# Collecting the spread of y about its first channel, and moving the sums of wo behind the first expert

## The chip, the cores and the metric

The kernel runs on one core of one Trainium2 chip. The metric is the device time of one execution in microseconds (us). The median of three runs of the kernel before is 2669.09 us (2668.46 to 2669.94). One more execution was taken with the hardware profiler; all rows shown come from it.

## The reference

All values are float32. There are B = 4 batches of S = 1024 tokens with D = 1024 channels. Cut to what matters:

```python
xn = layernorm(x)
# linear attention
q, v = xn @ Wq, xn @ Wv                    # 16 heads, lam = sigmoid(beta) per head
state[t] = lam * state[t-1] + v[t]         # along the tokens
y = q * state
mu, var = mean(y), var(y)                  # over the 1024 channels of a token
y = (y - mu) * rsqrt(var + 1e-5) * ln_g + ln_b
y = y * silu(xn @ Wg)
attention = y @ Wo
# mixture of 64 experts, top 8 per token, at most 128 tokens of an expert
w, idx = top8(softmax(xn @ router.T)), w / sum(w)
for each expert e, on its tokens xg:
    h = silu(xg @ w1[e]) * (xg @ v1[e])    # 384 hidden channels
    out[tokens] += w * (h @ w2[e])
x + attention + out
```

## The kernel before

**Layout.** In the attention, channels lie on the 128 partitions and tokens on the free axis. A channel group c of 128 channels (c = 0 to 7) is one tile y(c) of 128 x 1024, so the mean and the variance of a token are sums over eight tiles and then over 128 partitions. The sum over partitions is a matmul with a constant matrix whose elements are all 1/1024 (`all_channels`, L596 to L602, the tile `mean_w`); its result is the same in all partitions.

**Block products.** Every large product of matrices is done as a two by two block product with seven block products in place of eight. `left_sums` (L49 to L54) and `right_sums` (L57 to L68) form the sums and differences of blocks, `steps` (L130 to L175) runs the seven products: PSUM banks a, b and c take them, ACT copies partial results out (`copied`, L148: s1, s5 and s2), and DVE adds them (L160, L169, L172). A copy by ACT must be done before PE's next product may go on into the same bank: pc's second product waits for s5, and pa's next product for s2. `product` (L178) starts one product's first parts, finishes the product before (`before()`), and may put other work (`late`) ahead of its last parts.

**Per batch** (`batch_row`, L582). For m = 0 to 3, `states(m)` makes v and its scan and `queries(m)` multiplies q by it: this gives y(m) and y(m + 4). Then come four `gates(m)`, with silu of the gate, the layernorm of y (L680, L681, L684) and the DMAs of the gated y to DRAM (L689, from POOL's queue). `find_spread` (L655) is the `late` work of gates(0): it gives mean and 1/sqrt(var + eps).

**How the spread is collected before.** After queries(0) `find_shift` (L633) takes the mean of the first and fifth channel group, a quarter of the channels: POOL adds y(0) and y(4) (L644), PE sums over partitions (`sh`, two matmuls, L599), ACT scales (L636). This shift is subtracted from every y in place on DVE (L624). ACT squares the shifted y (L626, L629), POOL adds the squares into sum2 (L630) and the values into sum1 (L631). `find_spread` forms the mean from sum1, its square (L661), the variance from sum2 (L664), the root (L665, ACT, with a table load) and the reciprocal (L666, DVE). The shift keeps the difference of two large squares small.

**The experts** (`Experts`, L827). For expert e, `hidden(e)` runs the two products with w1 and v1 (L890), silu on ACT (L895) and the product on DVE (L896) into a tile of which there is one (tag "cur"). `fetch(e + 2)` loads the weights and gathers the tokens with indirect DMAs from POOL's queue (L857, L864). `turned(e + 1)` transposes the next tokens on DVE (L875). `output(e - 1)` transposes act on PE (hpt, L905), copies it (hT, L906, DVE), multiplies by w2 (L911), scales (L914) and adds to the output by an indirect DMA (L922). Between them stand the parts of the output projection y @ Wo (`project`, pa_o, pb_o, pc_o), 16 units spread over the experts. `load_wo` (L931) loads the four blocks of Wo and forms their sums on DVE at once.

**What sets the order.** A scheduler of the framework orders the instructions of each engine by its own estimates. Where `in_order` (L79) is used, the named engines keep the order of the program. For the first three experts that is DVE alone (L976). Semaphores between engines follow from the tiles that they share, and a tile that is to be reused waits for its last reader.

Of the kernel before, what the change touches and what calls it, by code (L numbers as in the profile page):

```python
# [8 lines left out]
F32 = mybir.dt.float32  # L9
I32 = mybir.dt.int32  # L10
AF = mybir.ActivationFunctionType
ALU = mybir.AluOpType
# [4 lines left out]
P = 128  # L17
B, S, D = 4, 1024, 1024
NTOK = B * S
KD = D // P  # L20
KH = KD // 2
SH = S // 2
NM = SH // P
# [22 lines left out]
H0, H1 = slice(0, SH), slice(SH, S)  # L46
# [10 lines left out]
def right_sums(eng, blocks, new, keep=False):  # L57


    t3 = blocks["T3"] = new("T3")  # L60
    eng.tensor_tensor(t3, blocks["B22"], blocks["B12"], ALU.subtract)
    b12 = blocks["B12"] if keep else blocks.pop("B12")
    t1 = blocks["T1"] = new("T1") if keep else b12
    eng.tensor_tensor(t1, b12, blocks["B11"], ALU.subtract)
    t2 = blocks["T2"] = new("T2")
    eng.tensor_tensor(t2, blocks["B22"], t1, ALU.subtract)
    t4 = blocks["T4"] = new("T4")
    eng.tensor_tensor(t4, blocks["B21"], t2, ALU.subtract)  # L68
# [29 lines left out]
class Pools:  # L98
# [21 lines left out]
    def y(self, name):  # L120
        return self.three.tile([P, 3, S], F32, tag="y", name=name)
# [111 lines left out]
def attn_and_routing(  # L233
# [3 lines left out]
    nc = tc.nc  # L237
    one, line, scratch, small = pools.one, pools.line, pools.scratch, pools.small
# [22 lines left out]
    eps = one.tile([P, 1], F32, name="eps")  # L261
# [320 lines left out]
    def batch_row(b, left):  # L582
# [3 lines left out]
        ys = [pools.y(f"y_{b}_{i}") for i in range(3)]  # L586

        def y(c, cols=slice(0, S)):
            return ys[place[c] // 3][:, place[c] % 3, cols]

        shift = mean = ys[2][:, 2, :]
        sum1 = one.tile([P, S], F32, tag="sum1", name=f"sum1_{b}")
        sum2 = one.tile([P, S], F32, tag="sum2", name=f"sum2_{b}")
        spread = []

        def all_channels(t, h, name):  # L596

            ps = pools.bank("r", [P, SH], name)
            nc.tensor.matmul(  # L599
                ps, lhsT=mean_w, rhs=t[:, h * SH : (h + 1) * SH], start=True, stop=True  # L600
            )
            return ps  # L602

        def states(m, left, late):

            lo = line.tile([P, S], F32, tag="line", name=f"lo_{b}_{m}")
            hi = line.tile([P, S], F32, tag="line", name=f"hi_{b}_{m}")

            def then(c21):
                scan(lo, lo, m, 0.0)  # L610
                scan(hi[:, H0], c21, m + KH, 0.0)
                scan(hi[:, H1], hi[:, H1], m + KH, hi[:, SH - 1 : SH])

            left = product(
                nc, pools, weights(b, 0, m), quarters[b],
                lo[:, H0], lo[:, H1], hi[:, H1], then, left, f"v_{b}_{m}", late,
                begun.get(0) if b == 0 and m == 0 else None,
            )
            return lo, hi, left

        def queries(m, lo, hi, left):
            def less_shift():
                for i, c in enumerate((m, m + KH)):
                    nc.vector.tensor_tensor(y(c), y(c), shift, ALU.subtract)  # L624
                    if m == 0 and i == 0:
                        nc.scalar.activation(sum2, y(c), AF.Square)  # L626
                        continue
                    sq = line.tile([P, S], F32, tag="line", name=f"sq_{b}_{c}")
                    nc.scalar.activation(sq, y(c), AF.Square)  # L629
                    nc.gpsimd.tensor_tensor(sum2, sum2, sq, ALU.add)  # L630
                    nc.gpsimd.tensor_tensor(sum1, y(0) if m == 0 else sum1, y(c), ALU.add)  # L631

            def find_shift():  # L633
                for h, cols in enumerate((H0, H1)):
                    ps = all_channels(sum1, h, f"sh_{b}_{h}")
                    nc.scalar.activation(shift[:, cols], ps, AF.Copy, scale=float(NM))  # L636
                less_shift()

            def then(c21):
                nc.vector.tensor_tensor(y(m + KH, H0), c21, hi[:, H0], ALU.mult)  # L640
                nc.vector.tensor_tensor(y(m), y(m), lo, ALU.mult)
                nc.vector.tensor_tensor(y(m + KH, H1), y(m + KH, H1), hi[:, H1], ALU.mult)
                if m == 0:
                    nc.gpsimd.tensor_tensor(sum1, y(0), y(KH), ALU.add)  # L644
                else:
                    less_shift()

            left = product(
                nc, pools, weights(b, 1, m), quarters[b],
                y(m, H0), y(m, H1), y(m + KH, H1), then, left, f"q_{b}_{m}", None,  # L650
                begun.get(1) if b == 0 and m == 0 else None,
            )
            return left, find_shift if m == 0 else None

        def find_spread():  # L655

            for h, cols in enumerate((H0, H1)):
                ps = all_channels(sum1, h, f"mean_{b}_{h}")
                nc.scalar.copy(mean[:, cols], ps)
            rstd = one.tile([P, S], F32, tag="sum1", name=f"rstd_{b}")  # L660
            nc.scalar.activation(rstd, mean, AF.Square)  # L661
            for h, cols in enumerate((H0, H1)):
                ps = all_channels(sum2, h, f"var_{b}_{h}")
                nc.vector.tensor_tensor(rstd[:, cols], ps, rstd[:, cols], ALU.subtract)  # L664
            nc.scalar.activation(rstd, rstd, AF.Sqrt, bias=eps)  # L665
            nc.vector.reciprocal(rstd, rstd)  # L666
            spread.append(rstd)

# [28 lines left out]
                find_spread if m == 0 else None,  # L697
            )

        late = None  # L700
        taking = take(b)
        for m in range(NM):
            lo, hi, left = states(m, left, late)
            if b == 0 and m == 0:
                for tokens in later:
                    store(*tokens)

                for to in (rows[NTOK:NROW, :], wtab[NTOK:NROW, :], out[NTOK:NROW, :]):
                    tc.keep_in_program_order(
                        nc.gpsimd.dma_start(out=to, in_=zero[:, 0 : to.shape[1]])  # L710
                    )
            next(taking)
            left, late = queries(m, lo, hi, left)
            next(taking)
            if b + 1 < B:
                if m == 1:
                    prep(b + 1, 0)
                elif m == 2:
                    load_turned(b + 1, 0)
                    route(b + 1, 0, folded(b + 1, 0, scored(b + 1, 0)))  # L720
            if m == NM - 1:
                tc.keep_in_program_order(
                    nc.sync.dma_start(
                        out=out[b * S : (b + 1) * S, :], in_=x[b * S : (b + 1) * S, :]
                    )
                )
# [3 lines left out]
        for m in range(NM):  # L730
# [8 lines left out]
            left = gates(m, left)  # L739
# [82 lines left out]
    for b in range(B):  # L822
        left = batch_row(b, left)
# [3 lines left out]
class Experts:  # L827
# [103 lines left out]
    def load_wo(self):  # L931
        for name, (i, o) in zip(("B11", "B21", "B22", "B12"), BLOCKS):
            self.wo_b[name] = self.pools.block(f"wo_{name}")
            load_block(self.nc, self.wo_b[name], self.wo, i, o * SH, SH)
        right_sums(self.nc.vector, self.wo_b, lambda n: self.pools.block(f"wo_{n}"))

    def load_gated(self, u):
        t = self.pools.left.tile([P, NSLOT, KH, P], F32, tag="w", name=f"gated_{u}")
# [23 lines left out]
        self.turn = self.turned(0)  # L962

    def run(self):
        units = B * NM
        gated = self.load_gated(0)
        self.fetch(1)
        self.load_wo()
        self.load(0, 2)


        begins = [1 + u * (E - 4) // units for u in range(units)] + [E - 3]
        before, todo, u, many = None, None, 0, iter(())
        for e in range(E):

            kept = [mybir.EngineType.DVE] if e < 3 else []  # L976
            with in_order(self.tc, kept):
                act = self.hidden(e, self.turn)
                self.fetch(e + 2)
                self.load(e + 1, 2)  # L980
                if e + 1 < E:
                    self.turn = self.turned(e + 1)
                if before is not None:
                    self.output(*before)
                before = e, act
                if u < units and e == begins[u]:
                    todo = self.project(u, gated)
                    many = iter((3, 2, 2) if begins[u + 1] - e == 3 else (2, 2, 2, 1))
                    u += 1
                    gated = self.load_gated(u) if u < units else None  # L990
                for _ in range(next(many, 0)):
                    next(todo, None)
        self.output(*before)
# [48 lines left out]
```

## Time and profile before

| what | value |
|---|---|
| median of three runs | 2669.09 us (2668.46 to 2669.94) |
| profiled execution | 2671.9 us, span 2670.1 us |
| mean granted clock of PE | 0.997 |
| PE busy | 2642.0 us, 99% |
| DVE busy | 1082.8 us, 41% |
| ACT busy | 330.8 us, 12% |
| POOL busy | 737.5 us, 28% |
| chain that ended last | PE 95%, DVE 3%, DMA 1% |

The span runs from the first to the last instruction of the profiled execution, and that execution's own time is 1.8 us longer. PE is the tensor engine, DVE the vector engine, ACT the scalar engine, POOL is GpSimd and SP issues DMAs. In a timeline row there are the start and the length in us, the engine, the line of the program, the operation, what it writes and reads, and in square brackets the idle time ahead of it with what ended it. In a group's row there are the busy time of all in us, the mean of one in ns and the idle time ahead. In a row of windows, after the stretch and its length, come the busy times of PE, PE's weight loads, DVE, ACT and POOL, with the number of instructions, and then the granted clock of PE, the share of the DMA engines and GB/s. A float32 matmul appears as two records.

### The profile page before, as it was taken

Reading aid. Unit: us, or ns where it says so; the run is one execution under the profiler, and the core shown is the slowest. Engines: PE = TensorE matmul, PEld = TensorE weight load, DVE = VectorE, ACT = ScalarE, POOL = GpSimd, SP = SyncE. Lnnn points to the kernel's source line nnn. Section 1 sums busy time; section 2 is a strip of 40 time slices with the busy share of each in tenths; the row PEclk is TensorE's granted clock in tenths of the full one; section 3 lists DMA queues with packets and bytes.
Section 4 is the critical chain, followed back from the end, with each engine's and each line's share of the span. In section 5 each row is a group of like instructions: output and inputs, shape, how many; then the busy total and the mean of one; then the engine's idle time right before and its main releaser. Section 6 shows DMA issues by size and latency. Waiting matters only on the chain.

```text
span 2670.1 us, 18675 instructions
## 1 busy us (share of the span) xinstructions
PE 2642.0 (99%) x6981; PEld 1272.4 (48%) x6981; DVE 1082.8 (41%) x1426; ACT 330.8 (12%) x492; POOL 737.5 (28%) x655
## 2 busy tenths in 40 slices
PE   9999999999999999999999999999999999999997
PEld 5444444444444444444555555555555555555554
DVE  7945676464943676373222212222122221222221
ACT  4213112131212211121000000000000000000000
POOL 1453312121122102132333323333233332333321
PEclk9999999999999999999999999999999999999999
DMA  6555534443335432326889888898888988889876
GB/s 236 194 182 194 193 107 144 179 156 110 123 110 210 166 116 83 145 98 239 296 284 305 283 274 284 285 304 283 274 284 284 305 283 273 284 286 303 270 272 181
DMA packets 122474, 592.95 MB, mean 222 GB/s; under 512 B 15872, under 2 KB 52736, under 8 KB 89360
## 3 DMA queue, kind: packets, MB, share of 16 engines
q1 hardware_dynamic: 81488, 448.03, 46.1%
q0 software_dynamic: 40464, 143.72, 19.9%
q8 instruction: 55, 0.90, 0.1%
q14 instruction: 35, 0.29, 0.0%
q10 hardware_dynamic: 432, 0.01, 0.0%
HBM read 483.67 MB, written 124.81 MB: 228 GB/s over the span
## 4 chain that ended last, share of the span: by engine, by line
PE 95%; DVE 3%; DMA 1%; issue 0%; ACT 0%; POOL 0%; SPq 0%; POOLq 0%; DVEq 0%; ACTq 0%
PE h L890 25%; PE y L911 12%; PE pa_o L137 8%; PE pa_g L137 8%; PE pa_v L137 7%; PE pa_q L137 7%; PE pc_o L137 4%; PE pc_q L137 4%; PE pc_g L137 4%; PE pc_v L137 4%; PE pb_g L137 2%; PE pb_o L137 2%; PE pb_v L137 2%; PE pb_q L137 2%; PE lg L475 1%; PE hpt L905 1%
## 5 line engine op out<-in xcount | busy, mean ns | idle before, releaser
L890 PE MATMUL h<-w,xgT 128*128 128x384 f32 x2048 | 672.2, 486 | 0.7 <-issue 0.7
L890 PEld LDWEIGHTS h<-w,xgT 128*128 128x128 f32 x2048 | 388.9, 190 | 286.1 <-issue 33.6
L857 POOL DMA_INDIRECT xg<-rows,tables x256 | 252.6, 987 | 669.4 <-DVE xgT L875 603.7
L911 PE MATMUL y<-w,hT 128*128 128x512 f32 x768 | 343.6, 597 | 1.6 <-DVE hT L906 1.6
L906 DVE COPY hT<-hpt 128x384 f32<-128x384 f32 x64 | 35.6, 557 | 724.5 <-PE hpt L905 724.5
L137 PE MATMUL pa_g<-xT,w 128*128 128x512 f32 x512 | 233.9, 600 | 2.9 <-DVE ghi L172 2.9
L911 PEld LDWEIGHTS y<-w,hT 128*128 128x128 f32 x768 | 140.9, 190 | 192.6 <-issue 153.3
L137 PE MATMUL pa_q<-xT,w 128*128 128x512 f32 x480 | 216.5, 593 | 2.0 <-DVE y L172 2.0
L137 PE MATMUL pa_v<-xT,w 128*128 128x512 f32 x480 | 217.4, 593 | 0.0
L137 PE MATMUL pa_o<-wo_T,gated 128*128 128x512 f32 x384 | 177.7, 592 | 0.0
L914 DVE TENSOR_SCALAR ys<-y,wt 128x512 f32<-128x512 f32 x128 | 95.9, 749 | 200.1 <-PE y L911 197.6
L137 PEld LDWEIGHTS pa_g<-xT,w 128*128 128x128 f32 x512 | 97.9, 192 | 127.3 <-issue 123.4
L137 PEld LDWEIGHTS pa_q<-xT,w 128*128 128x128 f32 x480 | 90.6, 190 | 114.6 <-issue 110.5
L137 PEld LDWEIGHTS pa_v<-xT,w 128*128 128x128 f32 x480 | 90.6, 190 | 114.5 <-issue 112.9
L895 ACT ACTIVATE act<-h 128x384 f32<-128x384 f32 x64 | 31.5, 492 | 848.5 <-PE hpt L905 833.2
L922 POOL DMA_INDIRECT out_dram<-ys,tables x63 | 102.5, 1627 | 112.0 <-DMA out_dram<-ohi 83.8
L689 POOL DMA_DIRECT2D gated<-y x64 | 48.2, 758 | 254.1 <-DVE y L684 242.3
L137 PE MATMUL pc_o<-wo_B,gated 128*128 128x512 f32 x256 | 117.1, 592 | 0.0
L137 PE MATMUL pc_g<-xT,w 128*128 128x512 f32 x256 | 115.3, 593 | 1.5 <-ACT sc_g L148 1.5
L137 PE MATMUL pc_v<-xT,w 128*128 128x512 f32 x256 | 115.4, 593 | 0.7 <-ACT sc_v L148 0.7
L137 PE MATMUL pc_q<-xT,w 128*128 128x512 f32 x256 | 115.5, 592 | 0.0
L631 POOL TENSOR_TENSOR sum<-sum,y 128x1024 f32<-128x1024 f32 x24 | 56.9, 2373 | 205.2 <-DVE y L624 205.2
(209 smaller groups left out, 2499.2 us busy)
## 6 DMA issues: line engine op xcount, KB each, us to landing
w<-in_w_dram SPq DMA_DIRECT2D x128, 1536.0 KB
w<-in_v_dram SPq DMA_DIRECT2D x64, 1536.0 KB
w<-wsum SPq DMA_DIRECT2D x36, 1792.0 KB
wsum<-w POOLq DMA_DIRECT2D x12, 1792.0 KB
x<-in_x_dram SPq DMA_DIRECT2D x32, 512.0 KB
rows<-x POOLq DMA_DIRECT2D x32, 512.0 KB
gated<-y POOLq DMA_DIRECT2D x64, 256.0 KB
gated<-gated SPq DMA_DIRECT2D x16, 1024.0 KB
```

The lines of the kernel that those rows point to most:

```text
L137: nc.tensor.matmul(ps, lhsT=lhs[:, slot, k, :], rhs=blocks[right][:, k, :], start=start and k == 0, stop=stop and k == KH - 1, skip_group_ ...
L475: nc.tensor.matmul(two[i * E : (i + 1) * E, :], lhsT=r_sb[:, i * KH + k, :], rhs=blocks[f"B{i + 1}{h + 1}"][:, k, :], start=(k == 0), stop ...
L631: nc.gpsimd.tensor_tensor(sum1, y(0) if m == 0 else sum1, y(c), ALU.add)
L689: nc.gpsimd.dma_start(out=gated[b, :, :, slot, m, :].rearrange("u p j -> p u j"), in_=yc[:, h * SH : (h + 1) * SH].rearrange("p (u j) -> p ...
L857: nc.gpsimd.indirect_dma_start(out=xg[:, r, :], out_offset=None, in_=self.rows.rearrange("n (q c) -> (n q) c", q=NQ), in_offset=bass.Indir ...
L890: nc.tensor.matmul(ps, lhsT=xT[:, k, :], rhs=w[:, k, :], start=(k == 0), stop=(k == KD - 1))
L895: nc.scalar.activation(act, ph[0], AF.Silu)
L905: nc.tensor.transpose(pt[:, j, :], act[:, j * P : (j + 1) * P], self.ident)
L906: nc.vector.tensor_copy(hT, pt)
L911: nc.tensor.matmul(ps, lhsT=hT[:, j, :], rhs=w2[:, j, cols], start=(j == 0), stop=(j == KF - 1))
L914: nc.vector.tensor_scalar(ys[:, cols], ps, wt, None, ALU.mult)
L922: self.nc.gpsimd.indirect_dma_start(out=to, out_offset=bass.IndirectOffsetOnAxis(ap=rows, axis=0), in_=ys, in_offset=None, compute_op=ALU.add,
```

## The change

Three things are changed.

1. The shift is gone. Each y(c) except y(0) has y(0) subtracted, on DVE, into a tile of its own (`away`), which is squared on ACT. POOL adds the squares into sum2 and the unshifted y into sum1. So in each partition the spread is collected about the value of that partition's first channel.
2. `find_spread` pools the partitions: from sum1 and y(0) it forms, with two subtractions on DVE and two squares on ACT, what has to be taken from and added to sum2 so that the sum over partitions is the variance about the common mean. The square of the mean and the subtraction from PSUM are gone; ACT takes the root from PSUM in two halves. In the changed kernel's own numbering the lines are: away L625, its square L626, the adds L628 and L629, the first off L650, its square L651, sum2 - off L652, the mean's matmuls and copies L655, the second off L656, its square L657, sum2 + off L658, var and its root L662, the reciprocal L663, and the subtraction of the mean from y L677.
3. The sums of the blocks of Wo move from `load_wo` into the first expert, behind the transposition of the second expert's tokens. For the first three experts PE is now kept in the order of the program, as DVE was.

```diff
--- before.py
+++ after.py
@@ -588,7 +588,7 @@
         def y(c, cols=slice(0, S)):
             return ys[place[c] // 3][:, place[c] % 3, cols]
 
-        shift = mean = ys[2][:, 2, :]
+        mean = ys[2][:, 2, :]
         sum1 = one.tile([P, S], F32, tag="sum1", name=f"sum1_{b}")
         sum2 = one.tile([P, S], F32, tag="sum2", name=f"sum2_{b}")
         spread = []
@@ -601,7 +601,7 @@
             )
             return ps
 
-        def states(m, left, late):
+        def states(m, left):
 
             lo = line.tile([P, S], F32, tag="line", name=f"lo_{b}_{m}")
             hi = line.tile([P, S], F32, tag="line", name=f"hi_{b}_{m}")
@@ -613,56 +613,53 @@
 
             left = product(
                 nc, pools, weights(b, 0, m), quarters[b],
-                lo[:, H0], lo[:, H1], hi[:, H1], then, left, f"v_{b}_{m}", late,
+                lo[:, H0], lo[:, H1], hi[:, H1], then, left, f"v_{b}_{m}", None,
                 begun.get(0) if b == 0 and m == 0 else None,
             )
             return lo, hi, left
 
         def queries(m, lo, hi, left):
-            def less_shift():
-                for i, c in enumerate((m, m + KH)):
-                    nc.vector.tensor_tensor(y(c), y(c), shift, ALU.subtract)
-                    if m == 0 and i == 0:
-                        nc.scalar.activation(sum2, y(c), AF.Square)
-                        continue
-                    sq = line.tile([P, S], F32, tag="line", name=f"sq_{b}_{c}")
-                    nc.scalar.activation(sq, y(c), AF.Square)
-                    nc.gpsimd.tensor_tensor(sum2, sum2, sq, ALU.add)
-                    nc.gpsimd.tensor_tensor(sum1, y(0) if m == 0 else sum1, y(c), ALU.add)
-
-            def find_shift():
-                for h, cols in enumerate((H0, H1)):
-                    ps = all_channels(sum1, h, f"sh_{b}_{h}")
-                    nc.scalar.activation(shift[:, cols], ps, AF.Copy, scale=float(NM))
-                less_shift()
+            def collect(c):
+
+                away = line.tile([P, S], F32, tag="line", name=f"away_{b}_{c}")
+                nc.vector.tensor_tensor(away, y(c), y(0), ALU.subtract)
+                nc.scalar.activation(sum2 if c == KH else away, away, AF.Square)
+                if c != KH:
+                    nc.gpsimd.tensor_tensor(sum2, sum2, away, ALU.add)
+                nc.gpsimd.tensor_tensor(sum1, y(0) if c == KH else sum1, y(c), ALU.add)
 
             def then(c21):
                 nc.vector.tensor_tensor(y(m + KH, H0), c21, hi[:, H0], ALU.mult)
                 nc.vector.tensor_tensor(y(m), y(m), lo, ALU.mult)
                 nc.vector.tensor_tensor(y(m + KH, H1), y(m + KH, H1), hi[:, H1], ALU.mult)
-                if m == 0:
-                    nc.gpsimd.tensor_tensor(sum1, y(0), y(KH), ALU.add)
-                else:
-                    less_shift()
+                for c in (m, m + KH):
+                    if c > 0:
+                        collect(c)
 
             left = product(
                 nc, pools, weights(b, 1, m), quarters[b],
                 y(m, H0), y(m, H1), y(m + KH, H1), then, left, f"q_{b}_{m}", None,
                 begun.get(1) if b == 0 and m == 0 else None,
             )
-            return left, find_shift if m == 0 else None
+            return left
 
         def find_spread():
 
+
+            off = line.tile([P, S], F32, tag="line", name=f"off_{b}")
+            nc.vector.scalar_tensor_tensor(off, y(0), -float(KD), sum1, ALU.mult, ALU.add)
+            nc.scalar.activation(off, off, AF.Square, scale=KD**-0.5)
+            nc.vector.tensor_tensor(sum2, sum2, off, ALU.subtract)
             for h, cols in enumerate((H0, H1)):
                 ps = all_channels(sum1, h, f"mean_{b}_{h}")
                 nc.scalar.copy(mean[:, cols], ps)
+            nc.vector.scalar_tensor_tensor(off, sum1, 1.0 / KD, mean, ALU.mult, ALU.subtract)
+            nc.scalar.activation(off, off, AF.Square, scale=KD**0.5)
+            nc.vector.tensor_tensor(sum2, sum2, off, ALU.add)
             rstd = one.tile([P, S], F32, tag="sum1", name=f"rstd_{b}")
-            nc.scalar.activation(rstd, mean, AF.Square)
             for h, cols in enumerate((H0, H1)):
                 ps = all_channels(sum2, h, f"var_{b}_{h}")
-                nc.vector.tensor_tensor(rstd[:, cols], ps, rstd[:, cols], ALU.subtract)
-            nc.scalar.activation(rstd, rstd, AF.Sqrt, bias=eps)
+                nc.scalar.activation(rstd[:, cols], ps, AF.Sqrt, bias=eps)
             nc.vector.reciprocal(rstd, rstd)
             spread.append(rstd)
 
@@ -697,10 +694,9 @@
                 find_spread if m == 0 else None,
             )
 
-        late = None
         taking = take(b)
         for m in range(NM):
-            lo, hi, left = states(m, left, late)
+            lo, hi, left = states(m, left)
             if b == 0 and m == 0:
                 for tokens in later:
                     store(*tokens)
@@ -710,7 +706,7 @@
                         nc.gpsimd.dma_start(out=to, in_=zero[:, 0 : to.shape[1]])
                     )
             next(taking)
-            left, late = queries(m, lo, hi, left)
+            left = queries(m, lo, hi, left)
             next(taking)
             if b + 1 < B:
                 if m == 1:
@@ -932,7 +928,6 @@
         for name, (i, o) in zip(("B11", "B21", "B22", "B12"), BLOCKS):
             self.wo_b[name] = self.pools.block(f"wo_{name}")
             load_block(self.nc, self.wo_b[name], self.wo, i, o * SH, SH)
-        right_sums(self.nc.vector, self.wo_b, lambda n: self.pools.block(f"wo_{n}"))
 
     def load_gated(self, u):
         t = self.pools.left.tile([P, NSLOT, KH, P], F32, tag="w", name=f"gated_{u}")
@@ -962,7 +957,7 @@
         self.turn = self.turned(0)
 
     def run(self):
-        units = B * NM
+        nc, units = self.nc, B * NM
         gated = self.load_gated(0)
         self.fetch(1)
         self.load_wo()
@@ -973,13 +968,15 @@
         before, todo, u, many = None, None, 0, iter(())
         for e in range(E):
 
-            kept = [mybir.EngineType.DVE] if e < 3 else []
+            kept = [mybir.EngineType.DVE, mybir.EngineType.PE] if e < 3 else []
             with in_order(self.tc, kept):
                 act = self.hidden(e, self.turn)
                 self.fetch(e + 2)
                 self.load(e + 1, 2)
                 if e + 1 < E:
                     self.turn = self.turned(e + 1)
+                if e == 0:
+                    right_sums(nc.vector, self.wo_b, lambda n: self.pools.block(f"wo_{n}"))
                 if before is not None:
                     self.output(*before)
                 before = e, act
```

## The prediction

> **What bounds the kernel now.** I read the engine shares first, then the chain of work that ended last.
>
> ```profile
> PE 2642.0 (99%) x6981; PEld 1272.4 (48%) x6981; DVE 1082.8 (41%) x1426; ACT 330.8 (12%) x492; POOL 737.5 (28%) x655
> ...
> PE 95%; DVE 3%; DMA 1%; issue 0%; ACT 0%; POOL 0%; SPq 0%; POOLq 0%; DVEq 0%; ACTq 0%
> ```
>
> TensorE is busy for 2642.0 of 2670.1 us. So an edit is worth what it takes from TensorE or from its few gaps, and it costs what it adds to either. Next I listed PE's gaps. Apart from the start and the tail, the ones above half a microsecond are 0.66, 1.48, 0.56, 1.00, 1.00, 0.68, 2.90, 0.71, 0.65, 0.65 and 0.98. The largest is in the timeline of PE and DVE where the attention hands over to the experts, and the window there shows the clock:
>
> ```profile
> 1242.53 2.29 DVE L61 TENSOR_TENSOR wo_T<-wo_B,wo_B 128x2048 f32<-128x2048 f32 x1 [10.23 <-DMA wo_B<-in_wo_dram]
> 1244.73 0.68 DVE L169 TENSOR_TENSOR glo<-pc_g,sc_g 128x512 f32<-128x512 f32 x1
> 1245.33 2.28 DVE L64 TENSOR_TENSOR wo_B<-wo_B,wo_B 128x2048 f32<-128x2048 f32 x1
> ...
> 1248.27 6.66 PE L137 MATMUL pa_g<-xT,w 128*128 128x512 f32 x8 [2.90 <-DVE ghi L172]
> ...
> 1248.00:1249.00 1.00, 0.73 (x1) 0.50 (x2) 1.00 (x2) 0.63 (x1) 0.00 (x0) 0.50 0.00 0
> 1250.00:1251.00 1.00, 1.00 (x3) 0.34 (x2) 1.00 (x1) 0.00 (x0) 1.00 (x2) 0.50 0.00 0
> ```
>
> DVE waits for the DMA of wo and then does its sums ahead of glo and ghi of the last gates; PE waits 2.90 us, and its next eight records last 6.66 us (3.43 elsewhere), at clock 0.50. By the clock of each microsecond, the half rate began about 1.9 us into the gap and lasted 6.85 us.
>
> **The change, part by part.**
>
> *The shift goes (gain).* The group to read is
>
> ```profile
> L599 PE MATMUL sh<-sum,mean_w 128*128 128x512 f32 x16 | 8.6, 616 | 0.0
> ```
>
> Sixteen records are eight matmuls. Eight records take 3.43 us in the chain, so a matmul takes 0.858 and eight take 6.87 us. No gap stands before them: **-6.87**. The eight ACT copies at L636, four of 32 subtractions at L624 and eight POOL adds (15 a batch become 13, 2.35 us each) go too. They run beside PE: nothing.
>
> *The pooled spread (loss).* The new find_spread (L650 to L663 and L677 below are the changed kernel's lines) adds on DVE `off` (L650), `sum2-off` (L652), a second `off` (L656) and `sum2+off` (L658), and two ACT squares (L651, L657); it drops the old square L661 and subtractions L664. DVE is 41% busy and ACT 12%, so the time itself hides. The queue positions do not. In the compiled order, in batches 1 and 2, ACT takes L651 ahead of its copies s5 (from pc_g) and s2 of the first gates; in batch 3 ahead of s2; in batch 0 behind both. L651 waits for `off`, which waits for POOL's last add to sum1, and behind it on ACT stand the copies that free PSUM for PE. Batch 1 before:
>
> ```profile
> 546.51 2.34 POOL L631 TENSOR_TENSOR sum<-sum,y 128x1024 f32<-128x1024 f32 x1
> 548.82 2.34 POOL L630 TENSOR_TENSOR sum<-sum,sq 128x1024 f32<-128x1024 f32 x1
> ...
> 548.88 3.43 PE pa_g L137 x8
> 552.31 3.43 PE pc_g L137 x8
> ```
>
> In the new order POOL's last sum1 add is the one that takes the place of 546.51, so it ends at 548.85, and the last add to sum2 follows at once, to 551.2. `off` reads two tiles from SBUF on DVE. What that meets is seen here:
>
> ```profile
> 237.14 5.87 DVE L624 TENSOR_TENSOR y<-y 128x1024 f32<-128x1024 f32 x1
> ...
> 236.67 2.34 POOL L630 TENSOR_TENSOR sum<-sum,sq 128x1024 f32<-128x1024 f32 x1
> 238.97 0.57 POOL L571 DMA_DIRECT2D wsum<-w  x1
> 239.55 2.37 POOL L631 TENSOR_TENSOR sum<-sum,y 128x1024 f32<-128x1024 f32 x1
> ```
>
> An operation of 1.22 us lasted 5.87, until POOL's adds were over. [...] If POOL starts first: `off` 551.2 to 552.5, square 1.06 to 553.6, s5's copy 0.59 to 554.15, against 552.31 when pc_g is due: 2.0 late, and 0.15 at var_0 (mean copy, L656, two subtractions L677 and L658 are 6.1 us, against 6.0 of matmuls placed there). If DVE starts first: 551.8, in time. POOL needs no semaphore from another engine there, so I take it as first: 2.15 each, **+4.3** for batches 1 and 2 (ends 0.3 and 4.3).
>
> Batch 3: POOL works through the token DMAs until 1162.27, so sum1 is ready at 1164.65, and pa_g is due at 1165.66:
>
> ```profile
> 1162.28 2.37 POOL L631 TENSOR_TENSOR sum<-sum,y 128x1024 f32<-128x1024 f32 x1
> 1164.58 2.38 POOL L630 TENSOR_TENSOR sum<-sum,sq 128x1024 f32<-128x1024 f32 x1
> ...
> 1165.66 1.88 PE L137 MATMUL pa_g<-xT,w 128*128 128x512 f32 x4
> ```
>
> POOL first: 1167.0, `off` 1168.3, square 1169.35, copy 1169.95: 4.3, with 0.4 at var_0 **+4.7** (DVE first: 2.0 and 0.4). Batch 0: its 1.48 and 0.56 stay; POOL's weight sums (1.26 each) delay `off` and the second chain by 0.3 to 2.0; I take **+1.3**. The later reciprocal (6.55 us, same as before) leaves over 4 us to the first gated product: nothing.
>
> *The sums of wo (gain, then loss).* The four sums (2.29 each, 9.2 us) move behind xgT of expert 1, under its hidden product of 10.4 us: hidden, with 1.1 us to spare; past that each us would delay act of expert 1 by as much. Their loads keep their place on SP. The gap of 2.90 and the slow phase (6.66 - 3.43 = 3.23) go: **-6.13**.
>
> But PE is now kept in written order for experts 0 to 2. Before, PE did this:
>
> ```profile
> 1264.68 0.55 PE L905 MATMUL hpt<-ident,act 128*128 128x128 f32 x3 [0.71 <-DVE act L896]
> 1265.88 10.56 PE L890 MATMUL h<-w,xgT 128*128 128x384 f32 x32 [0.65 <-issue]
> 1276.27 2.74 PE L137 MATMUL pa_o<-wo_B,gated 128*128 128x512 f32 x6
> 1278.85 2.32 PE L911 MATMUL y<-w,hT 128*128 128x512 f32 x5
> ```
>
> hpt (the transposes of act) stood in a gap, and pa_o covered the wait for hT. Now hpt of expert 0 comes after the hidden product of expert 1, and y directly behind it. The act tile has one buffer, so the next silu waits for hpt: hpt 0.33, silu 0.49, act 0.55, xgT 1.24, hT 0.52 and releases (0.2) give 3.35 us until y, 3.0 of them idle: **+3.35**. One expert later one matmul of h fills in: **+2.5** by the same chain. The gap of 1.92 around hpt stays, now unbroken.
>
> *The clock.* The gaps are 2.0, 2.0 and 4.3 in the attention, 1.9, 3.0 and 2.5 at the experts. The row of 2.90 lost 3.23. Gaps up to 1.48 kept clock 1.00. [...]
>
> *Sum.* -6.87 + 4.3 + 4.7 + 1.3 - 6.13 + 3.35 + 2.5 + 8.2 = +11.3 on the profiled execution of 2671.9 (span 2670.1 and 1.8 around it), 2683.2. That execution stands 2.8 above the median 2669.09, so **2680.4**. [...]
>
> **Rivals.**
> [...]
> [...]
> 3. Slower still: every gap of 2 us loses 3.2 as well, or w2 of expert 0, whose tile is freed by gated's DMAs (now behind four token DMAs of POOL), lands after y of expert 0 is due (I estimate 2 us to spare): **2690**.
>
> **How the numbers follow.** Forecast 0.55, rival 1 0.22, rival 2 0.13, rival 3 0.10. Measurement can tell about 0.2%, 5.3 us: below 2663.8 is faster, above 2674.4 slower. Slower: 0.47 of the forecast, 0.05 of rival 1, 0.10: 0.62. Faster: 0.13. The rest, 0.25, is the same. The likeliest case alone spans 2673 to 2688; the range reaches to 2664 and 2690.
>
> **What would show it.** Right: no sh rows; PE gaps behind ACT sc_g near 2 us in batches 1 and 2 and near 4 in batch 3, with L650 stretched beyond 1.3 us; no gap behind ghi; gaps of 3.0 and 2.5 ahead of y behind hT in experts 0 and 1, followed by slices at clock 0.50. Wrong: L650 at 1.3 us and no sc_g gap (rival 1 or 2), clock 1.00 behind the gaps, or sums of wo that stretch past the hidden product.

## The result and the profile after

The changed kernel takes 2683.7 us (median of five runs, 2683.0 to 2684.56) against 2668.46 us for the kernel before (five runs, 2667.8 to 2669.94, the three quoted earlier among them): a ratio of 1.0055, 95% interval 1.0045 to 1.0066. It is slower by 15.2 us. Its profiled execution has a span of 2681.9 us, 11.8 more than the one of before.

The shares, from the page of the changed kernel:

```profile
PE 2640.8 (98%) x6965; PEld 1271.6 (47%) x6965; DVE 1100.7 (41%) x1430; ACT 326.3 (12%) x488; POOL 744.3 (28%) x647
...
PE 92%; DVE 4%; issue 1%; POOL 1%; ACT 1%; DMA 1%; POOLq 0%; DVEq 0%; ACTq 0%
```

TensorE's busy time fell by only 1.2 us although 6.9 us of matmuls are gone, and its share of the chain fell from 95% to 92%. What took their place stands in the view of what PE waited for (the total in us, how often, and the longest):

```profile
PE pc_g L137 <- ACT sc_g L148: 4.6, 3, 1.5
PE y L907 <- DVE hT L902: 4.4, 3, 2.8
PE h L886 <- issue: 4.3, 2, 2.4
PE pa_g L137 <- ACT sc_g L148: 3.8, 1, 3.8
PE pc_v L137 <- ACT sc_v L148: 2.4, 1, 2.4
...
PE mean L599 <- POOL sum L629: 1.8, 2, 1.2
PE mean L599 <- ACT y L655: 1.7, 1, 1.7
```

The wait for ghi is no longer there. PE's gaps above a quarter of a microsecond add up to 27.1 us; they were 13.9 (2.1 of each at the start). To these 13.2 us come the half-rate stretches, that is the stretches in which the granted clock of PE is 0.50 in place of 1.00. In the one of before eight records that take 3.43 us elsewhere took 6.66, so I count half of the time that PE works in them as lost: 7.4 us now (behind the gaps of 2.43, 3.83, 1.92 and 2.37), 3.0 before, so 4.4 more. With the shift's 6.9 us taken off that is 10.7; about 1 of the 11.8 us is not located.

### The profile page after: what moved, and what is told of

Same layout as the page of the kernel before. It is cut to its first block, busy times and chain, and to the rows that moved or that the text cites. A ratio compares the mean times of both kernels' runs of the same rounds, so it can differ in the third digit from the quotient of the medians.

```text
span 2681.9 us, 18628 instructions
## 1 busy us (share of the span) xinstructions
PE 2640.8 (98%) x6965; PEld 1271.6 (47%) x6965; DVE 1100.7 (41%) x1430; ACT 326.3 (12%) x488; POOL 744.3 (28%) x647
## 4 chain that ended last, share of the span: by engine, by line
PE 92%; DVE 4%; issue 1%; POOL 1%; ACT 1%; DMA 1%; POOLq 0%; DVEq 0%; ACTq 0%
PE h L886 24%; PE y L907 13%; PE pa_o L137 8%; PE pa_g L137 7%; PE pa_v L137 7%; PE pa_q L137 7%; PE pc_o L137 4%; PE pc_q L137 4%; PE pc_v L137 4%; PE pc_g L137 3%; PE pb_o L137 2%; PE pb_g L137 2%; PE pb_q L137 2%; PE pb_v L137 2%; PE lg L475 1%
## 5 line engine op out<-in xcount | busy, mean ns | idle before, releaser
L629 POOL TENSOR_TENSOR sum<-sum,y 128x1024 f32<-128x1024 f32 x24 | 72.6, 3024 | 267.9 <-DVE y L633 231.1
```

Source lines behind the costliest of these rows:

```text
L629: nc.gpsimd.tensor_tensor(sum1, y(0) if c == KH else sum1, y(c), ALU.add)
```

## The experiments

All times are medians; the ratio is against the kernel before on the same chip, with its 95% interval. The runs fell on several chips, on which the kernel before itself differs by up to 1.4 us. So where I compare with the changed kernel I use how much each is above its own before; the changed kernel is 15.2 above.

| kernel | us | before | ratio |
|---|---|---|---|
| e1_wo_alone | 2675.4 | 2669.86 | 1.0021 (1.0013 to 1.0029) |
| e2_spread_alone | 2677.41 | 2669.86 | 1.0031 (1.002 to 1.0042) |
| e3_pe_free | 2674.47 | 2669.86 | 1.0017 (1.0008 to 1.0025) |
| e4_act_order | 2679.01 | 2669.86 | 1.0038 (1.0024 to 1.0052) |
| e5_last_add_dve | 2680.7 | 2669.9 | 1.0042 (1.0028 to 1.0056) |
| e6_mean_first | 2703.4 | 2669.9 | 1.0123 (1.0106 to 1.014) |
| e7_late_collect | 2679.7 | 2669.9 | 1.0036 (1.0022 to 1.005) |
| e8_all | 2694.56 | 2669.9 | 1.0089 (1.0072 to 1.0106) |
| e9_last_on_dve | 2659.78 | 2669.19 | 0.9967 (0.9955 to 0.9979) |
| e10_wo_pe_free | 2665.77 | 2669.19 | 0.9987 (0.998 to 0.9993) |

### The two halves apart: e1 and e2

e1 is the kernel before with the third part alone:

```diff
-        right_sums(self.nc.vector, self.wo_b, ...)        # in load_wo
-            kept = [mybir.EngineType.DVE] if e < 3 else []
+            kept = [mybir.EngineType.DVE, mybir.EngineType.PE] if e < 3 else []
...
+                if e == 0:
+                    right_sums(nc.vector, self.wo_b, ...)   # behind turned(e + 1)
```

> The kernel before with the third part alone: wo's sums inside expert 0, and PE kept in program order for three experts. Theory (the gain at ghi is paid back by the waits of y for hT): the gap of 2.90 and its slow phase go (-2.9 and up to -3.4), gaps of 2.8 and 2.4 ahead of y or h come (+5.5 with hpt), and slow phases of 1.7 each at one to three of the gaps: between 1 faster and 5 slower than before, about 2671. Rival (the third part is the whole loss, the spread costs nothing): 2680 or more. Rival (the third part gains 6): 2662.

Measured: 5.5 us slower than before, just past the theory's upper end of 5. PE's gaps there are those of the changed kernel: 1.92, 2.76 and 2.37.

e2 is the changed kernel with these lines put back, so that only the spread differs from before.

> The kernel before with the first two parts alone: the spread about the first channel, pooled; wo's sums and PE's order as before. Theory: four matmuls' worth of shift pairs is gone (-6.9), but PE's gaps in the attention grow from 5.4 to 16.3 and two slow phases come (1.7 and about 3): +7 to +9 on before, 2676 to 2678. The two halves together should give the whole change, 2683.7. Rival (all the loss is at the experts): 2661 to 2663.

Measured: 7.6 us slower, as expected; both rivals that put the whole loss in one half fall. Together the halves lose 13.1 us, and the whole change 15.2; the 2.1 us between are not explained.

### The order of PE at the experts: e3 and e10

e3 is the changed kernel with one word taken out; e10 is e1 with the same word taken out:

```diff
-            kept = [mybir.EngineType.DVE, mybir.EngineType.PE] if e < 3 else []
+            kept = [mybir.EngineType.DVE] if e < 3 else []
```

> The changed kernel with PE left to the scheduler in the first three experts; the sums of wo stay inside expert 0 and DVE is kept in order. Theory (the order of PE makes the gaps ahead of y): hpt of expert 0 goes back between the two hidden products and pa_o covers hT; the gaps of 2.77 and 2.37 and their slow phase go, the gap of 1.92 is broken by hpt and loses no clock: 5 to 9 less than the changed kernel, 2675 to 2679. Rival (the sums on DVE are what delays y): gaps of 2 to 3 stay ahead of y, 2683.

> The kernel before with wo's sums inside expert 0, DVE in order as before and PE left to the scheduler. Theory (the move itself gains the gap at ghi and its slow phase, and only PE's order gave it back): 4 to 6 less than the kernel before, 2664 to 2666. Rival (moving the sums makes new waits by itself): 2669 or more.

Measured: e3 is 4.6 us slower than before instead of 15.2 (a little more was won than the theory's 5 to 9), and e10 is 3.4 us faster (less than the theory's 4 to 6), where e1 with PE in order was 5.5 slower. So keeping PE in order costs 9 us in one pair and 11 in the other, and the move of the sums alone gains 3.4. The timeline of PE in the changed kernel:

```profile
1268.31 12.25 PE L886 MATMUL h<-w,xgT 128*128 128x384 f32 x32 [1.92 <-issue]
1280.40 0.49 PE L901 MATMUL hpt<-ident,act 128*128 128x128 f32 x3
1283.66 0.70 PE L907 MATMUL y<-w,hT 128*128 128x512 f32 x1 [2.77 <-DVE hT L902]
```

and in e3:

```profile
1267.00 0.55 PE L901 MATMUL hpt<-ident,act 128*128 128x128 f32 x3 [0.71 <-DVE act L892]
1268.20 10.56 PE L886 MATMUL h<-w,xgT 128*128 128x384 f32 x32 [0.66 <-issue]
1278.59 2.74 PE L137 MATMUL pa_o<-wo_B,gated 128*128 128x512 f32 x6
1281.17 2.32 PE L907 MATMUL y<-w,hT 128*128 128x512 f32 x5
```

In e3 hpt breaks the first gap and pa_o covers hT. The rival, that the sums of wo delay y, falls with e3 and with DVE's timeline of the changed kernel: the sums end 4.09 us before the next product on DVE starts, and that product waits for silu:

```profile
1275.07 2.29 DVE L68 TENSOR_TENSOR wo_T<-wo_B,wo_T 128x2048 f32<-128x2048 f32 x1
1281.45 0.55 DVE L892 TENSOR_TENSOR act<-act,h 128x384 f32<-128x384 f32 x1 [4.09 <-ACT act L891]
1281.92 1.24 DVE L871 STREAM_TRANSPOSE xgT<-xg 128x1024 f32<-128x1024 f32 x1
1283.09 0.52 DVE L902 COPY hT<-hpt 128x384 f32<-128x384 f32 x1
```

### The place of off's square on ACT: e4

```diff
-            left = gates(m, left)
+            with in_order(tc, [mybir.EngineType.Activation] if m == 0 else []):
+                left = gates(m, left)
```

> The changed kernel with ACT kept in program order inside the first gates of each batch: the only difference is that the square of the first off stands behind the copies s5 and s2 on ACT in batches 1, 2 and 3. Theory (its place in ACT's queue holds PE back): the gaps of 1.54, 1.54 and 3.83 behind sc_g go and with the last its slow phase: 7 to 10 less than the changed kernel, 2674 to 2677; off itself stays at 3.36 us. Rival (DVE and POOL are late as such, so the wait only moves to var): the gaps reappear ahead of var, 2682 to 2684.

Measured: 2679.01, 9.2 us above before and so some 6 less than the changed kernel, not 7 to 10. In batches 1 and 2 the theory holds: the two gaps of 1.54 are gone. In batch 3 the rival holds in another place, at mean and not at var:

```profile
1162.40 1.13 PE L599 MATMUL mean<-sum,mean_w 128*128 128x512 f32 x2 [1.23 <-POOL sum L629]
1163.36 1.88 PE L137 MATMUL pa_g<-xT,w 128*128 128x512 f32 x4
1170.38 2.08 PE L599 MATMUL mean<-sum,mean_w 128*128 128x512 f32 x2 [5.13 <-ACT y L655]
```

The second mean waits until ACT has copied the first out of PSUM, and that copy still stands behind the square and behind silu of glo, whose sum stands behind off on DVE. So in batches 1 and 2 the square's place in the queue was the cause; in batch 3, where sum1 itself is late, moving it back in one queue only moved the wait to what stands behind it.

### POOL's add and the length of off: e5

```diff
-                    nc.gpsimd.tensor_tensor(sum2, sum2, away, ALU.add)
+                    (nc.vector if c == KD - 1 else nc.gpsimd).tensor_tensor(sum2, sum2, away, ALU.add)
```

> The changed kernel with the last add into sum2 of each batch on DVE instead of POOL, so that POOL has no add behind its last one into sum1. [...] Rival (off is slow by itself): it stays at 3.36 and the time at 2684.

Measured: 2680.7, 10.8 above before and so some 4 us less than the changed kernel. I had foreseen 5 to 8 less, off at 1.3 us, no gaps of 1.54 in batches 1 and 2 and one of about 1.8 in batch 3. In batches 1 to 3 off falls from 3.36 us to 1.21 to 1.23 without POOL's add beside it, so the cause of its length is shown, and the gap of batch 3 falls from 3.83 to 1.69 as foreseen; but those of batches 1 and 2 only fall to 0.96 and 0.95, and one of 1.50 came ahead of var in batch 0. The timeline of DVE in e5 says why (POOL's row below it):

```profile
549.19 3.36 DVE L628 TENSOR_TENSOR sum<-sum,away 128x1024 f32<-128x1024 f32 x1 [2.66 <-POOL sum L628]
552.47 0.68 DVE L160 TENSOR_TENSOR glo<-pb_g,sc_g 128x512 f32<-128x512 f32 x1
553.07 1.21 DVE L650 SCALAR_TENSOR_TENSOR off<-y,sum 128x1024 f32<-128x1024 f32 x1
...
549.12 2.34 POOL L629 TENSOR_TENSOR sum<-sum,y 128x1024 f32<-128x1024 f32 x1
```

The add that went to DVE now lasts 3.36 us itself, against POOL's add into sum1 that began 0.07 us earlier, and off stands behind it. The collision moved by one operation.

### Mean first: e6

The two loops over the halves of mean go ahead of the first off, and ACT and DVE are both kept in order in the first gates:

```diff
+            for h, cols in enumerate((H0, H1)):
+                ps = all_channels(sum1, h, f"mean_{b}_{h}")
+                nc.scalar.copy(mean[:, cols], ps)
             off = line.tile([P, S], F32, tag="line", name=f"off_{b}")
...
+            with in_order(tc, [mybir.EngineType.Activation, mybir.EngineType.DVE] if m == 0 else []):
+                left = gates(m, left)
```

> The changed kernel with the matmuls and copies of the mean ahead of the first off, and ACT and DVE in program order inside the first gates, so that glo's sum and the mean's copies stand ahead of off and its square. Theory (in batch 3 it is off's place in the queues of DVE and ACT that holds mean_1 back): no gap behind sc_g in batches 1 to 3 and none of 3 to 5 us at mean_1; the gap of 1.2 ahead of mean_0 stays since sum1 is late; 7 to 11 less than the changed kernel, 2673 to 2677. Rival (the correction is too long a chain wherever it stands): gaps of 2 us and more ahead of var, 2680 or more.

Measured: 2703.4, 33.5 above before and so worse by 18 us than the changed kernel. The theory failed, and the rival named the wrong place. The gaps behind sc_g are gone, none above 0.37 came at var, and one of 3.80 came ahead of mean in batch 0. But with DVE in written order the reciprocal stands ahead of ghi's sum, and the last block product of the first gates, which goes into the bank that this sum reads, comes behind products of the next gates. It ends at 594.80; only then, at 594.83, is the load issued that takes the place of the first gates' weights (in the changed kernel at 576.45), and PE waits for it, in batches 1 and 2 (4.14 in batch 2). It is the order of DVE that does this: in e4, which keeps ACT alone in order, ghi's sum runs at 560.75, ahead of the reciprocal at 573.43, and no product waits for weights. Batch 1 of e6:

```profile
583.54 6.55 DVE L663 RECIPROCAL rstd<-rstd 128x1024 f32<-128x1024 f32 x1 [1.26 <-ACT rstd L662]
590.01 0.63 DVE L172 TENSOR_TENSOR ghi<-pa_g,sc_g 128x512 f32<-128x512 f32 x1
...
596.07 3.70 PE L137 MATMUL pa_g<-xT,w 128*128 128x512 f32 x8 [1.28 <-DVE ghi L172]
603.88 6.72 PE L137 MATMUL pa_g<-xT,w 128*128 128x512 f32 x8 [4.11 <-DMA w<-wsum]
```

### The gap in batch 0: e7

The gap of 2.43 ahead of pc_v was in no forecast. e7 gives out away, the square and the adds of batch 0 behind the partial copies of the next product, with ACT in order there:

```diff
-                for c in (m, m + KH):
-                    if c > 0:
-                        collect(c)
+                if b > 0 or m == NM - 1:
+                    collect_both()
...
-            lo, hi, left = states(m, left)
+            with in_order(tc, [mybir.EngineType.Activation] if b == 0 and m > 0 else []):
+                lo, hi, left = states(m, left, late)
```

> The changed kernel where, in batch 0, away, its square and the adds are given out behind the partial copies of the next product, with ACT in program order there. Theory (the gap of 2.43 ahead of pc_v is ACT's copy standing behind a square that waits for DVE's backlog): the gap falls to 0.5 or less and its slow phase goes: 2 to 4 less than the changed kernel, 2680 to 2682. Rival (PE waits for something else there): the gap stays, 2684.

Measured: 2679.7, 9.8 above before and so some 5 us less than the changed kernel, a little more than the theory's 2 to 4. The gap and its half-rate stretch are gone. In ACT's timeline the square had stood between pc_v and its copy; in e7 it comes behind both copies. The changed kernel first, then e7:

```profile
140.14 1.06 ACT L626 ACTIVATE away<-away 128x1024 f32<-128x1024 f32 x1 [9.32 <-DVE away L625]
141.10 0.57 ACT L148 COPY sc_v<-pc_v 128x512 f32<-128x512 f32 x1
```

```profile
136.45 0.59 ACT L148 COPY sc_v<-pc_v 128x512 f32<-128x512 f32 x1 [9.71 <-PE pc_v L137]
139.88 0.58 ACT L148 COPY sc_v<-pa_v 128x512 f32<-128x512 f32 x1 [2.85 <-PE pa_v L137]
140.37 2.12 ACT L626 ACTIVATE away<-away 128x1024 f32<-128x1024 f32 x2
```

Before the change the same copy ran at 141.48 and PE waited 0.66. PE has come 2.15 us earlier (its product pc_v began at 132.36, before at 134.51), but DVE was working off the search for each expert's tokens (MAX8 and MATCH_REPLACE8 without a pause up to 138), so away and its square came only 0.38 earlier. Here the matmuls of the shift were removed in front of an engine that was about to be waited for anyway.

### All together, twice: e8 and e9

e8 joins the edits of e3, e5, e6 and e7.

> The changed kernel with all of it: mean first with ACT and DVE in program order in the first gates, the last add into sum2 on DVE, the late collection in batch 0, and PE left to the scheduler in the first experts. Theory: the shift's matmuls (-6.9) and the wait for wo (-2.9 and its slow phase) are gone and little comes in their place: 2657 to 2664, faster than the kernel before. Rival (the pieces meet elsewhere): 2667 or more.

Measured: 2694.56. It carries e6's harm (waits for weights of 4.03 and 4.08, and gaps of 3.72 and 3.49 ahead of mean in batches 0 and 3), and the theory of a sum of gains fails with it.

e9 leaves the order of the first gates to the scheduler, keeps the edits of e3 and e7, and puts both last adds on DVE:

```diff
+                eng = nc.vector if c == KD - 1 else nc.gpsimd
                 if c != KH:
-                    nc.gpsimd.tensor_tensor(sum2, sum2, away, ALU.add)
-                nc.gpsimd.tensor_tensor(sum1, y(0) if c == KH else sum1, y(c), ALU.add)
+                    eng.tensor_tensor(sum2, sum2, away, ALU.add)
+                eng.tensor_tensor(sum1, y(0) if c == KH else sum1, y(c), ALU.add)
```

> The changed kernel with the last adds of each batch into sum1 and sum2 both on DVE (in batch 3 POOL's is behind the token DMAs), the late collection in batch 0, and PE left to the scheduler in the first experts; the order inside the first gates is the scheduler's. Theory: off is ready before the copies are due, so no gap behind sc_g in batches 1 to 3, none of 1.2 at mean_0 of batch 3, none ahead of y; only those of batch 0's first gates and of 1.0 stay: 2655 to 2661, faster than the kernel before by 0.3 to 0.5%. [...]

Measured: 2659.78 us, ratio 0.9967 (0.9955 to 0.9979): 9.4 us faster than the kernel before, as expected, and 25 less than the changed one. In batch 3 the last add no longer waits behind the token DMAs of POOL, and off is ready before the copy is due:

```profile
1149.47 1.22 DVE L630 TENSOR_TENSOR sum<-sum,y 128x1024 f32<-128x1024 f32 x1
...
1152.34 1.22 DVE L655 SCALAR_TENSOR_TENSOR off<-y,sum 128x1024 f32<-128x1024 f32 x1
```

In the changed kernel off began at 1167.03, about 11 us after y(7) was there; here it is 4 us. PE's gaps above a quarter of a microsecond add up to 11.1 us, and no half-rate stretch stands before the tail. Beside e10, which ran on the same chip and has the old spread with the sums of wo moved and PE free, e9 is 6.0 us faster: most of the 6.9 us of matmuls that the idea takes away. How much of this the two adds on DVE bring was not tried alone. The queues that it used were what cost.

### The clock: e11, the changed kernel once more

> The changed kernel once more, for its trace. Theory (the clock is judged in windows of 3.41 us whose phase has nothing to do with the kernel; a window with more than about 1.8 us without a matmul is followed by one at half rate): the gaps are the same to 0.1 us, but the half-rate stretches may stand behind others of them; each gap that puts 1.9 or more into one window has one behind it, none with less than 1.7 in each. Rival (the gap's length decides): half-rate stretches behind exactly the same four gaps.

The gaps came out the same to 0.02 us, and the half-rate stretches did not. In the first trace one stands behind the gap of 1.92, ahead of the hidden product of expert 1, and none behind that of 2.77, ahead of y. The clock is the third column from the right; the gaps end at 1268.31 and 1283.66:

```profile
1267.00:1268.00 1.00, 0.00 (x0) 0.00 (x0) 1.00 (x2) 0.00 (x0) 0.00 (x0) 1.00 0.72 303
1269.00:1270.00 1.00, 1.00 (x3) 0.39 (x3) 1.00 (x1) 0.00 (x0) 1.00 (x1) 0.50 0.86 319
...
1283.00:1284.00 1.00, 0.34 (x1) 0.30 (x2) 0.61 (x2) 0.00 (x0) 0.57 (x1) 1.00 0.93 377
1284.00:1285.00 1.00, 1.00 (x3) 0.38 (x2) 0.00 (x0) 0.00 (x0) 0.70 (x2) 1.00 0.97 406
```

In e11 the same two gaps end at 1267.95 and 1281.60, and it is the other way round:

```profile
1269.00:1270.00 1.00, 1.00 (x5) 0.60 (x4) 1.00 (x1) 0.00 (x0) 1.00 (x1) 1.00 1.03 418
1282.00:1283.00 1.00, 1.00 (x2) 0.39 (x2) 0.00 (x0) 0.00 (x0) 0.70 (x2) 0.50 0.99 377
```

So the length of a gap alone doesn't decide, and the rival falls. The theory holds but for one window: the gap of 1.92 lies wholly in one in e11 by the records, ends less than 0.1 us before its edge, and has no half rate behind it.

## Why the prediction was right, and where it was not

The forecast was slower, 2680.4 us in a range of 2664 to 2690; measured 2683.7. The sum on the profiled execution was +11.3, measured +11.8. By its own steps:

- **The shift, -6.87.** The matmuls are gone, but the step took their time for gained everywhere because no gap stood ahead of them. In batch 0 the gap ahead of pc_v grew from 0.66 to 2.43 and drew a half-rate stretch of 3.4 us, 1.7 us lost: 3.5 us given back. e7 shows the cause. This term was missing.
- **Batches 1 and 2, 2.15 each.** Measured 1.54 each, and nothing at var. It came about as foretold: POOL's next add began at 550.51, off at 550.57, and off lasted 3.36 us.

```profile
550.51 2.34 POOL L628 TENSOR_TENSOR sum<-sum,away 128x1024 f32<-128x1024 f32 x1
...
550.57 3.36 DVE L650 SCALAR_TENSOR_TENSOR off<-y,sum 128x1024 f32<-128x1024 f32 x1 [2.61 <-POOL sum L629]
...
553.97 1.06 ACT L651 ACTIVATE off<-off 128x1024 f32<-128x1024 f32 x1 [6.82 <-DVE off L650]
554.93 0.57 ACT L148 COPY sc_g<-pc_g 128x512 f32<-128x512 f32 x1
...
555.55 3.70 PE L137 MATMUL pc_g<-xT,w 128*128 128x512 f32 x8 [1.54 <-ACT sc_g L148]
```

- **Batch 3, 4.7.** Measured 3.83 behind sc_g and 1.25 ahead of mean_0, 5.1 together. The second was not foretold: POOL's token DMAs ended at 1164.63, later than the 1162.27 that I carried over from before, so sum1 came later too.

```profile
1163.67 0.96 POOL L853 DMA_INDIRECT xg<-rows,tables  x1 [0.30 <-issue]
1164.65 2.35 POOL L629 TENSOR_TENSOR sum<-sum,y 128x1024 f32<-128x1024 f32 x1
```

- **Batch 0's spread, 1.3.** Measured 1.68, ahead of the second mean.
- **The wait for wo, -6.13.** The gap is gone. But e10 gains only 3.4 in the median: the slow phase of 3.23 was in the profiled execution of before and need not be in the others, and in e2 the same wait (2.46 there) has no half rate behind it.
- **PE in written order, +3.35 and +2.5.** Measured 2.77 with hpt's 0.33 ahead of it, and 2.37. e3 and e10 put the whole of it, with the clock, at 9 to 11 us; with the 2.9 and 3.1 that I gave the clock there, the forecast of it was 11.9.
- **The clock, +8.2.** This term was an estimate of mine, from the length of a gap and the 6.85 us at half rate that the gap of 2.90 drew before, and no run shows it. By the records it is 7.4, so the total came out near and its parts did not: I put 2.2, 2.9 and 3.1 behind three gaps (4.3, 3.0 and 2.5), and it was 1.7, 2.3, 1.7 and 1.7 behind four (2.43, 3.83, 1.92 and 2.37), while 2.77 went free. To go by the nearest row in length was wrong, as e11 shows: the gap of 1.92 lost the clock in the first trace and not in e11, and 2.77 in e11 and not in the first. That the sum agreed is partly luck.
- **The median, -2.8.** This step failed too. I carried the profiled execution's distance from the median over to the changed kernel. The changed kernel's profile (2681.9 and 1.8) is at its median exactly. Before, the execution stood 3.4 above the median of five runs, about what its half-rate stretch cost. That this is the cause is argued, not shown; the runs of before in the experiments agree with it: of 22 below 2669 us 20 have a mean granted clock of 0.998, and of 27 above 2670 us 23 have 0.997. Without this step the forecast would have been 2683.2.

Rival 1, with off done in time because DVE starts first, fell at off's 3.36. Rival 2, faster, was not this kernel. e9 shows its idea: with the correction ready before the copies are due the time is 2659.78, though e9 also leaves PE free at the experts. Rival 3's late load of w2 did not occur; its other half came in part, since the gaps of 1.92, 2.37 and 2.43 did lose the clock, but 1.7 us each and not 3.2.

## What to carry to other kernels

When TensorE is 98% busy, cost an edit by what stands in front of each small copy that frees PSUM, on every in-order queue: in batches 1 and 2 an added square of 1.06 us, which hides as work, held PE for 1.54 us by its place. Removing matmuls pays only where the engine that PE meets next is early enough. And keep PE's order free where fillers cover a chain over ACT and DVE; one word there was worth 9 to 11 us.

## What the runs showed of the hardware

- **In these traces the half-rate stretches lie on a grid.** In the traces of before, of the changed kernel, of e11 and of e8 each stretch at clock 0.50 ahead of the tail lasts 3.41 or 6.83 us. Within a trace their starts lie whole multiples of 3.413 us apart: in the changed kernel 1027.41, 98.99 and 44.37 us, which are 301, 29 and 13 of them. The phase of the grid differs between two traces of one kernel: a stretch starts at 1268.75 in the changed kernel's first trace and one at 1281.68 in e11, 3.79 steps later. In the four traces, from 20 us on and ahead of the tail, 13 windows of this grid at full rate were followed by one at half rate; each holds 1.92 us or more without a matmul. About 50 others that hold a gap of a quarter of a microsecond or more were not, and all of them hold 1.7 us or less, but for the one of 1.92 in e11 that ends at the edge. In e11 a window that held 1.25 us of one gap and 0.88 of the next was followed by half rate: there the sum counted. The gap of 2.77 ahead of y, cut by an edge into 1.5 and 1.3, cost nothing in the first trace and 1.7 us in e11, where the 5.42 us of matmuls behind it lasted 7.11. Whether the spread between runs of one kernel comes from this was not shown.
- **A half-rate stretch lasted one window or two in these four traces.** Two where the first window at half rate itself held 0.84 us or more without a matmul (6 cases), one where it held 0.40 or less (7 cases).
- **An operation of DVE that the first of two POOL adds released, with the second just begun, lasted 3.36 us** each time: off in batches 1 to 3 (3.36 us; 1.21 to 1.23 in e5, where that second add is not on POOL), and in e5 the add that went to DVE (3.36 us; 1.22 in e9). POOL's add, begun 0.06 to 0.09 us ahead, took its 2.34 or 2.35 us.
